# Keeping the node states of eight blocks in attention-only memory between two graph layers

## The chip, the cores and the metric

The kernel runs on one core of one Trainium2 chip. The metric is device time in microseconds (us), the median over runs of the whole program; lower is better.

The core has five engines, each with its own instruction queue. TensorE (PE, with its weight loads shown as PEld) does matrix products and transposes. VectorE (DVE) and ScalarE (ACT) do elementwise work. GpSimd (POOL) here issues the gathers and scatters, the DMAs that take row numbers from a table. SyncE (SP) issues plain DMAs. 16 DMA engines carry out what all of them issue. SBUF is the on-chip memory in 128 partitions, PSUM holds TensorE's results, HBM ("DRAM" in the code) is the memory beside the chip.

## The reference

Eight independent inputs of 2048 nodes with 128 features, all over one sparse graph (each possible edge is there with probability 1/128), pass through four layers. Layers 0 and 1 are attention over the neighbours with a feed-forward network behind it; layers 2 and 3 are graph attention with one score per edge. The text counts layers from 0, so the third and fourth layer are layers 2 and 3. Cut to what matters:

```python
# layers 0 and 1 (8 heads of 16)
Q, K, V = h @ Wq, h @ Wk, h @ Wv
attn = softmax(where(adj == 0, -inf, Q K^T / 4))
x = layer_norm(h + attn V @ Wo + bo) * g1 + b1
x = layer_norm(x + relu(x @ W1 + b1) @ W2 + b2) * g2 + b2
# layers 2 and 3
h = x @ W
e = leaky_relu(h @ a_src [i] + h @ a_dst [j], 0.2)
att = softmax(where(adj == 0, -inf, e))
y = att @ h + x                       # x, the layer's input, is added again
x = gamma * (y - mean(y)) * rsqrt(var(y) + 1e-5) + beta
```

A layer's input is thus needed twice: for its projection, and at the end of the layer, where it is added to the result. That input is what the text calls a state.

## The kernel before

**Sparse rows.** The start of the program sorts the nodes by their number of neighbours and makes a list of neighbours for each. Nodes are then worked on in 16 blocks of 128, from the most neighbours to the fewest (29 list places for block 0, 10 for block 15). Each layer has a table in HBM with one row per node, all eight inputs side by side: keys and values for layers 0 and 1 (8 KB a row), projected features and two exponentials for layers 2 and 3 (4160 bytes a row).

**Chunks.** A block's list is cut into chunks of at most 2 places (layers 0 and 1) or 4 (layers 2 and 3). For each place one gather (`gather`, L302, GpSimd) brings the rows of 128 neighbours into one of seven buffers `kv`. In layers 2 and 3 (`gat_chunk`) VectorE multiplies seven of eight inputs by the edge weights (L818), ScalarE the eighth (L823), in layer 2 VectorE also adds one pair of places (L829), and TensorE sums the places into `acc` (L316). `fetch` issues the gathers of up to five chunks ahead.

**Block ends.** After its last chunk a block has a tail (`tail`, `outputs` L703, `gat_tail`). In layer 2 it adds the state (`center` times `xT`, L852), normalizes (ACT L860, L868), transposes back, writes the new state over the old one in `xT` (L494), projects it for layer 3 (L520) and copies the result into `rows` (ACT L530), of which there is one buffer. In layer 3 it normalizes into `n`, scales and shifts it (DVE L898, L900) and writes it to the output (L902). Tails run in small steps between the chunks of the next block.

**States.** When both halves of a block are done, `state_done` stores the state to `kept[t]` in HBM (L551, SyncE), writes `rows` into the next layer's table (L507, GpSimd) and asks for the state that is needed next: block t+4 of the same layer, or of the next layer at the end (`load_state`, L298, SyncE). There are four state tiles `xT`, so a load waits until its tile's earlier block is stored and no longer read. All 16 states are stored and loaded between any two layers.

**Order.** The program's order on every engine is the order in which the Python code emits it; no scheduler moves instructions. What an engine waits for is set by semaphores derived from the tiles' use. SyncE takes its DMAs strictly in that order: one that waits holds back all behind it.

**Memory that the change touches.** The weights of layers 0 and 1 (`w_L0_...`, `w_L1_...`: `qkv`, `o`, `W1`, `w2`, together 4 KB per partition and layer), `ring` (exponentials of attention), `block_sum` (softmax sums of attention), and the pool tiles tagged `xn`, `hT` and `q`, used by attention (`q` also by layer 3's `n`, two buffers). A state takes 4 KB per partition.

Of the kernel before, what the change touches and what calls it, by code (L numbers as in the profile page):

```python
# [9 lines left out]
F32 = mybir.dt.float32  # L10
# [8 lines left out]
P = 128  # L19
B, N, D = 8, 2048, 128  # L20
# [3 lines left out]
FF = 256  # L24
# [5 lines left out]
NB = 8  # L30
# [4 lines left out]
STATES = 4  # L35
# [54 lines left out]
def sparse_path(ctx: ExitStack, tc: tile.TileContext, ins: dict, out: bass.AP, flag: bass.AP):  # L90
# [10 lines left out]
    nc = tc.nc  # L101
    const = ctx.enter_context(tc.tile_pool(name="const", bufs=1))
    work = ctx.enter_context(tc.tile_pool(name="work", bufs=2))
# [6 lines left out]
    def misc():  # L110
        return pm.tile([P, 512], F32, tag="m", name="m")
# [33 lines left out]
    bufs = [const.tile([P, CHUNK], F32, name=f"kv{i}") for i in range(KVB)]  # L145
    turn = [-1]
    ring = const.tile([P, RING, P], F32, name="ring")
# [7 lines left out]
    kept = [dram.tile([P, B * P], F32, name=f"kept{t}") for t in range(NT)]  # L155
# [19 lines left out]
    block_sum = const.tile([P, NT, NB * NH], F32, name="block_sum")  # L175
# [5 lines left out]

    waiting = []

    def load(name, shape):
        t = const.tile(shape, F32, name=f"w_{name}")
        if name == "L0_qkv":
            nc.scalar.dma_start(t, ins[name])
        else:
            waiting.append((t, ins[name]))
        return t  # L190
# [11 lines left out]
    def row(name, n):  # L202
        t = line(n)
        waiting.append((t, ins[name].rearrange("p a b -> p (a b)") if n > D else ins[name]))
        return t

    W = {}
    for l in (0, 1):
        W[l] = {
            "qkv": load(f"L{l}_qkv", [P, 384]),  # L210
            "o": load(f"L{l}_o", [P, D]),
            "1": load(f"L{l}_gnn_W1", [P, FF]),
            "2": load(f"L{l}_w2", [P, 2, D]),
            "col": load(f"L{l}_col", [P, 7]),
            "row": row(f"L{l}_row", 4 * D).rearrange("p (a b) -> p a b", b=D),
        }
# [76 lines left out]
    def state_tile():  # L293
        return work.tile([P, B, P], F32, tag="xT", name="xT", bufs=STATES)

    def load_state(t):
        xT = state_tile()
        nc.sync.dma_start(xT.rearrange("p b n -> p (b n)"), kept[t])  # L298
        return xT

# [14 lines left out]
    def turn_into(dst, src, start):  # L315
        nc.tensor.matmul(  # L316
            dst, src, ident, start=start, stop=True, is_transpose=True, skip_group_check=True
        )

    def transpose4(src):  # L320
        pt = misc()
        for j in range(4):
            nc.tensor.transpose(pt[:, j * P : (j + 1) * P], src[:, j, :], ident)  # L323
        return pt.rearrange("p (b c) -> p b c", c=P)
# [145 lines left out]
    def inverse_roots(ss):  # L470

        rs = small.tile([P, ss.shape[-1]], F32, tag="rs", name="rs", bufs=3)
        nc.scalar.activation(rs, ss, AF.Ln)
        nc.scalar.activation(rs, rs, AF.Exp, scale=-0.5)
        return rs
# [17 lines left out]
    def affine(dst, src, col):  # L493
        nc.scalar.activation(dst, src, AF.Identity, scale=col[:, 0:1], bias=col[:, 1:2])  # L494
# [11 lines left out]
    def put_rows(l, t, rows, dst=None):  # L506
        return nc.gpsimd.indirect_dma_start(  # L507
            out=tables[l][:, :] if dst is None else dst,
            out_offset=bass.IndirectOffsetOnAxis(ap=perm[:, t : t + 1], axis=0),
            in_=rows[:, : width(l)], in_offset=None,  # L510
        )
# [33 lines left out]
    def state_done(l, t, box):  # L545


        box["halves"] = box.get("halves", 0) + 1
        if box["halves"] == 2:
            if l < 3:  # L550
                nc.sync.dma_start(kept[t], box["x"].rearrange("p b n -> p (b n)"))  # L551
                dst = views[l + 1][max(0, t - (NT - LATE) + 1)]
                assert len(puts[l + 1]) == t
                puts[l + 1].append(put_rows(l + 1, t, box["rows"], dst).ins)
                put[l + 1] += 1
            box["done"] = True
            state(l, t + STATES)
# [165 lines left out]
    def rows_of(box):  # L723
        if "rows" not in box:
            box["rows"] = work.tile([P, NB * 2 * D], F32, tag="rows", name="rows", bufs=1)
        return box["rows"]

    def attention_tail(l, t, box, i):
# [54 lines left out]
        yield from project(l + 1, i, xT, rows_of(box), t)  # L783
        yield
        state_done(l, t, box)

    def gat_chunk(l, c):
# [43 lines left out]
        add_up(acc, hv, k, left, c["folded"])  # L833
        yield

    def gat_tail(l, t, box):

        wt = W[l]
        xT = box["x"]
        if l == 2:  # L840
            ns = [work.tile([P, 4, D], F32, tag="n", name="n2") for _ in range(2)]
        else:
            n = work.tile([P, NB, D], F32, tag="q", name="n")
            ns = [n[:, :4, :], n[:, 4:, :]]
        ys = [None, None]
        rs = [None, None]

        def added(h):
            ys[h] = y = misc().rearrange("p (b c) -> p b c", c=D)
            for j in range(4):  # L850
                turn_into(y[:, j, :], box["o"][:, 4 * h + j, :], j == 0)
                nc.tensor.matmul(  # L852
                    y[:, j, :], xT[:, 4 * h + j, :], center, start=False, stop=True,
                    skip_group_check=True,
                )

        def squares(h):
            ss = small.tile([P, 4], F32, tag="ss", name="ss", bufs=3)
            for j in range(4):
                nc.scalar.activation(  # L860
                    ns[h][:, j, :], ys[h][:, j, :], AF.Square, bias=eps, scale=D**-0.5,
                    accum_out=ss[:, j : j + 1],
                )
            rs[h] = inverse_roots(ss)

        def scaled(h):
            for j in range(4):
                nc.scalar.mul(ns[h][:, j, :], ys[h][:, j, :], rs[h][:, j : j + 1])  # L868

        def half_rows(h):  # L870
            scaled(h)
            yield
            pt = transpose4(ns[h])
            yield
            affine(xT[:, 4 * h : 4 * h + 4, :], pt, wt["col"][:, 0:2])
            yield
            yield from project(3, 4 * h, xT, rows_of(box), t)
            yield
            state_done(l, t, box)

        def half_done(h):
            added(h)
            yield
            squares(h)
            yield
            if l == 2:
                yield from half_rows(h)
            else:
                scaled(h)

        halves = [half_done(0), later(2, lambda: half_done(1))]
        while halves:
            advance(halves)
            yield
        if l == 3:
            for _ in range(3):
                yield
            nc.vector.tensor_mul(n, n, last_g[:, None, :].to_broadcast([P, B, D]))  # L898
            yield
            nc.vector.tensor_add(n, n, last_b[:, None, :].to_broadcast([P, B, D]))  # L900
            yield
            nc.gpsimd.indirect_dma_start(  # L902
                out=out, out_offset=bass.IndirectOffsetOnAxis(ap=perm[:, t : t + 1], axis=0),
                in_=n.rearrange("p b d -> p (b d)"), in_offset=None,
            )
            state_done(l, t, box)
            state_done(l, t, box)
# [235 lines left out]
    every = []  # L1143
    blocks = [[{} for _ in range(NT)] for _ in range(4)]
    for l in range(4):
        per = 2 if l < 2 else 4
        for t, k, ns, folded in pieces(l, per):
            c = dict(l=l, t=t, k=k, ns=ns, folded=folded, box=blocks[l][t])
# [8 lines left out]
    def advance(group):  # L1157
        for g in list(group):
            if next(g, 0) == 0:
                group.remove(g)  # L1160
# [40 lines left out]
    def later(n, make):  # L1201
        for _ in range(n):
            yield
        yield from make()

    def tail(l, t, box):
        for _ in range(4 if l < 2 else 3 if t > NT - 4 else 5):
            yield
        outputs(l, t, box)
        if l < 2:  # L1210
            tails.append(later(1, lambda: attention_tail(l, t, box, 0)))
            tails.append(later(4, lambda: attention_tail(l, t, box, 4)))
        else:
            tails.append(later(1, lambda: gat_tail(l, t, box)))
        yield

    def state(l, t):
        if t >= NT:
            l, t = l + 1, t - NT
        if 0 < l < 4:  # L1220
            blocks[l][t].update(x=load_state(t), ready=True)

    def begin(c):
        if c["l"] < 2:
# [610 lines left out]
```

## Time and profile before

| | |
|---|---|
| median of 3 runs | 2802.78 us (2800.01 to 2805.45) |
| the profiled execution | 2808.35 us, its span 2806.6 us |
| busy: PE, DVE, ACT, POOL | 84%, 90%, 49%, 63% |
| DMA | 982.02 MB, mean 350 GB/s |
| first store of a state of layer 2 | 2018.75 us |
| last load of a state of layer 3 | 2717.55 us |

The span is the time from the first to the last instruction in the profile; the execution's own time has a little around it. Times inside the profile are counted from the span's start. A row of a timeline has the start in us, the duration in us, engine, line, operation, output and input; in brackets stands the idle time of the engine before it and who ended it. A row of waits has the waiting engine and line, what it waited for, the total in us, the number of times and the longest. `issue` as a releaser means that the profile shows no wait.

In windows of the profile, layer 2's chunks run from about 1894 to 2350 us and layer 3's from about 2356 to 2766 us, with the first chunks of a layer beside the last tails of the one before.

### The profile page before, as it was taken

The numbers are of one execution on the slowest core, as the hardware profiler recorded it, in microseconds if no ns is written. First come the engines' busy times: TensorE is split into PE (matmuls) and PEld (weight loads), VectorE is DVE, ScalarE is ACT, GpSimd is POOL, SyncE is SP. The second block draws the span as 40 slices with busy tenths as digits, with TensorE's granted clock in tenths as the row PEclk, the third lists the DMA queues.
The fourth block names the chain that finished last, engine by engine and source line by source line (L and its number), as shares of the span: only waits on it lengthen the run. The fifth ranks groups of instructions, "written<-read, shape, count | busy, mean of one in ns | idle before, by whom it ended". The sixth has DMA issues, their size and how long they took to land.

```text
span 2806.6 us, 48937 instructions
## 1 busy us (share of the span) xinstructions
PE 2349.6 (84%) x17811; PEld 2130.1 (76%) x17811; DVE 2513.9 (90%) x2467; ACT 1381.9 (49%) x5032; POOL 1774.4 (63%) x1346
## 2 busy tenths in 40 slices
PE   5866898898899998798989999997767887788885
PEld 4655787787788887688878888886667786787785
DVE  9697999999999887999999999985989997799895
ACT  3611444454555665154445555565445565445554
POOL 3377788778656455546565665573776775677772
PEclk9978999999999999999999999999788888999997
DMA  9898899999989888789999999985999998999994
GB/s 368 274 370 318 358 335 331 386 334 363 382 325 365 326 329 317 304 311 367 357 386 367 354 378 363 355 324 175 382 412 385 401 409 332 349 411 413 400 413 166
DMA packets 197730, 982.02 MB, mean 350 GB/s; under 512 B 30268, under 2 KB 32060, under 8 KB 125488
## 3 DMA queue, kind: packets, MB, share of 16 engines
q0 software_dynamic: 172080, 885.06, 82.0%
q1 hardware_dynamic: 20650, 68.39, 6.3%
q10 hardware_dynamic: 4752, 25.36, 2.7%
q8 instruction: 143, 2.34, 0.3%
q14 instruction: 105, 0.86, 0.1%
HBM read 921.28 MB, written 91.55 MB: 361 GB/s over the span
## 4 chain that ended last, share of the span: by engine, by line
PE 37%; DVE 27%; DMA 15%; issue 10%; ACT 8%; POOL 2%; POOLq 0%; ACTq 0%; DVEq 0%
PE acc L316 13%; DMA kv<-table,lists 11%; DVE kv L675 9%; DVE kv L637 8%; PE pair L316 4%; PE m L773 3%; PE m L756 3%; DVE kv L818 3%; PE m L520 2%; PE m L323 2%; PE m L768 2%; PE m L573 2%; PE m L739 1%; PE m L743 1%; POOL kv L302 1%
## 5 line engine op out<-in xcount | busy, mean ns | idle before, releaser
L302 POOL DMA_INDIRECT kv<-table,lists x938 | 1305.5, 1392 | 669.3 <-PE acc L316 288.0
L316 PE MATMUL acc<-ident,kv 128*128 128x128 f32 x8048 | 1059.2, 286 | 166.5 <-DVE kv L675 90.3
L316 PEld LDWEIGHTS acc<-ident,kv 128*128 128x128 f32 x8048 | 964.3, 148 | 230.0 <-DVE kv L675 114.4
L637 DVE TENSOR_TENSOR kv<-kv,q 128x2048 f32<-128x2048 f32 (+1 forms) x280 | 617.9, 2207 | 37.2 <-DMA kv<-table,lists 26.6
L675 DVE TENSOR_TENSOR kv<-kv,weights 128x2048 f32<-128x2048 f32 (+1 forms) x282 | 625.9, 2220 | 25.1 <-ACT weights L667 24.8
L818 DVE TENSOR_TENSOR kv<-kv,pair 128x3584 f32<-128x3584 f32 (+1 forms) x150 | 530.7, 3538 | 1.0
L316 PE MATMUL pair<-ident,kv 128*128 128x128 f32 (+1 forms) x2256 | 300.2, 277 | 87.4 <-issue 75.4
L643 DVE TENSOR_TENSOR kv<-kv 128x1024 f32<-128x1024 f32 (+1 forms) x282 | 334.9, 1187 | 9.2
L316 PEld LDWEIGHTS pair<-ident,kv 128*128 128x128 f32 (+1 forms) x2256 | 255.8, 140 | 107.8 <-issue 88.3
L302 POOL DMA_INDIRECT kv<-table,sorted_lists x150 | 195.7, 1304 | 139.2 <-PE acc L316 40.8
L659 ACT ACTIVATE ring<-pair 128x128 f32<-128x128 f32 (+1 forms) x282 | 77.7, 276 | 366.5 <-PE pair L316 302.2
L823 ACT ACTIVATE kv<-kv,ws 128x128 f32<-128x128 f32 x544 | 174.7, 397 | 153.3 <-DVE ws L812 144.0
L667 ACT COPY weights<-pair 128x128 f32<-128x128 f32 (+1 forms) x282 | 73.3, 260 | 357.1 <-PE pair L663 351.4
L483 ACT ACTIVATE n<-m,eps 128x128 f32<-128x128 f32 x512 | 181.6, 371 | 135.0 <-PE m L773 130.7
L860 ACT ACTIVATE n<-m,eps 128x128 f32<-128x128 f32 x256 | 90.8, 374 | 182.2 <-PE m L852 180.0
L773 PE MATMUL m<-w_L_w,hT 128*128 128x128 f32 x1024 | 156.4, 275 | 0.0
L490 ACT ACTIVATE n<-m,rs 128x128 f32<-128x128 f32 x512 | 146.4, 376 | 0.3
L773 PEld LDWEIGHTS m<-w_L_w,hT 128*128 128x128 f32 x1024 | 135.1, 192 | 0.0
L756 PE MATMUL m<-n1T,w_L_gnn_W 128*128 128x512 f32 x256 | 132.5, 602 | 3.0 <-ACT hT L761 1.8
L703 DVE TENSOR_TENSOR o<-acc,scale 128x512 f32<-128x512 f32 x128 | 83.2, 683 | 50.5 <-ACT scale L721 27.0
L520 PE MATMUL m<-w_L_h,xT 128*128 128x130 f32 x512 | 84.8, 298 | 46.5 <-ACT xT L494 29.3
L323 PE MATMUL m<-ident,n 128*128 128x128 f32 x640 | 113.4, 290 | 11.9 <-ACT n L490 5.6
(233 smaller groups left out, 3593.2 us busy)
## 6 DMA issues: line engine op xcount, KB each, us to landing
kept<-xT SPq DMA_DIRECT2D x48, 512.0 KB, 6.7
xT<-kept SPq DMA_DIRECT2D x48, 512.0 KB, 7.0
kv<-in_adj_dram SPq DMA_DIRECT2D x16, 1024.0 KB, 15.8
table<-kv ACTq DMA_DIRECT2D x16, 1024.0 KB, 4.5
kv<-table,lists POOLq DMA_INDIRECT x938, 8.8
kv<-in_x_nodes_dram ACTq DMA_DIRECT2D x16, 512.0 KB, 11.1
kv<-table,sorted_lists POOLq DMA_INDIRECT x150, 6.7
found<-kv POOLq DMA_DIRECT2D x16, 64.0 KB, 5.6
```

The lines of the kernel that those rows point to most:

```text
L302: this = nc.gpsimd.indirect_dma_start(out=dst, out_offset=None, in_=tables[l][:, :] if need == NT else views[l][0], in_offset=bass.Indirec ...
L316: nc.tensor.matmul(dst, src, ident, start=start, stop=True, is_transpose=True, skip_group_check=True)
L323: nc.tensor.transpose(pt[:, j * P : (j + 1) * P], src[:, j, :], ident)
L483: nc.scalar.activation(dst[:, i, :], z[:, i, :], AF.Square, bias=eps, scale=D**-0.5, accum_out=ss[:, i : i + 1],)
L490: nc.scalar.mul(dst[:, i, :], z[:, i, :], rs[:, i : i + 1])
L637: nc.vector.tensor_mul(kk, kk, q[:, None].to_broadcast([P, ns, NB, D]))
L643: nc.vector.tensor_add(hk.rearrange("p j (c h) -> p c j h", h=NH), kj[:, :, :NH, :], kj[:, :, NH:, :])
L675: nc.vector.tensor_mul(vv, vv, w.rearrange("p (s b h) -> p (s b) h", b=NB, h=NH)[:, :, None, :] .to_broadcast([P, ns * NB, HD, NH]),)
L756: nc.tensor.matmul(ph, wt["1"][:, f * P : (f + 1) * P], n1T.rearrange("p b c -> p (b c)"), start=True, stop=True,)
L773: nc.tensor.matmul(y[:, j, :], hT[:, f, j, :], wt["2"][:, f, :], start=False, stop=f == 1, skip_group_check=True,)
L818: nc.vector.tensor_mul(hv[:, :, :nv, :], hv[:, :, :nv, :], wc[:, :, :nv, None].to_broadcast([P, ns, nv, D]))
L823: nc.scalar.mul(hv[:, i, b, :], hv[:, i, b, :], ws[:, i, b - nv : b - nv + 1])
```

## The change

The states of blocks 4 to 11 are loaded in layer 2 into eight places of their own, called homes: the weights of layer 0, `ring`, `block_sum`, the tiles `xn` and `hT`, both tiles `q`, and the weights of layer 1. Layer 2 updates them there, and layer 3 reads them there; their store in layer 2 and their load in layer 3 are left out (8 of each, 512 KB apiece). Blocks 0 to 3 and 12 to 15 go through `kept` as before. So that weights can hold a state, the four weight tiles of a layer become slices of one tile `every`. Layer 3's output `n`, which used the `q` tiles, goes into two halves of one tile `ends` with the tag `rows`, in turn.

```diff
+    def load(name, shape, t=None):
+        if t is None:
+            t = const.tile(shape, F32, name=f"w_{name}")
...
     for l in (0, 1):
+        every_w = const.tile([P, NB * D], F32, name=f"w_L{l}")
         W[l] = {
-            "qkv": load(f"L{l}_qkv", [P, 384]),
-            "o": load(f"L{l}_o", [P, D]),
-            "1": load(f"L{l}_gnn_W1", [P, FF]),
-            "2": load(f"L{l}_w2", [P, 2, D]),
+            "every": every_w,
+            "qkv": load(f"L{l}_qkv", None, every_w[:, :384]),
+            "o": load(f"L{l}_o", None, every_w[:, 384 : 384 + D]),
+            "1": load(f"L{l}_gnn_W1", None, every_w[:, 512 : 512 + FF]),
+            "2": load(f"L{l}_w2", None, every_w[:, 768:].rearrange("p (f d) -> p f d", d=D)),
...
+    def flat(tile):
+        return tile.rearrange("p (b n) -> p b n", n=P)
+
+    homes = [
+        lambda: flat(W[0]["every"]),
+        lambda: ring[:, :B, :],
+        lambda: flat(block_sum.rearrange("p t c -> p (t c)")),
+        lambda: work.tile([P, B, P], F32, tag="xn", name="home", bufs=1),
+        lambda: flat(work.tile([P, 2, 4, P], F32, tag="hT", name="home", bufs=1)
+                     .rearrange("p f b c -> p (f b c)")),
+        lambda: work.tile([P, B, P], F32, tag="q", name="home"),
+        lambda: work.tile([P, B, P], F32, tag="q", name="home"),
+        lambda: flat(W[1]["every"]),
+    ]
+    STAY = range(STATES, STATES + len(homes))
+
-    def load_state(t):
-        xT = state_tile()
+    def load_state(l, t):
+        xT = homes[t - STATES]() if l == 2 and t in STAY else state_tile()
         nc.sync.dma_start(xT.rearrange("p b n -> p (b n)"), kept[t])
...
             if l < 3:
-                nc.sync.dma_start(kept[t], box["x"].rearrange("p b n -> p (b n)"))
+                if l < 2 or t not in STAY:
+                    nc.sync.dma_start(kept[t], box["x"].rearrange("p b n -> p (b n)"))
...
+    ends = []
+
     def gat_tail(l, t, box):
...
-            n = work.tile([P, NB, D], F32, tag="q", name="n")
+            if not ends:
+                ends.append(work.tile([P, NB * 2 * D], F32, tag="rows", name="ends", bufs=1))
+            n = ends[0][:, t % 2 * NB * D : (t % 2 + 1) * NB * D].rearrange("p (b d) -> p b d", d=D)
...
-        if 0 < l < 4:
-            blocks[l][t].update(x=load_state(t), ready=True)
+        if l == 3 and t in STAY:
+            blocks[3][t].update(x=blocks[2][t]["x"], ready=True)
+        elif 0 < l < 4:
+            blocks[l][t].update(x=load_state(l, t), ready=True)
```

More of the change, by code (lines that the diff above doesn't have):

```diff
@@ L182, in sparse_path @@
     waiting = []
-    def load(name, shape):
-        t = const.tile(shape, F32, name=f"w_{name}")
+    def load(name, shape, t=None):
+        if t is None:
+            t = const.tile(shape, F32, name=f"w_{name}")
         if name == "L0_qkv":
```

## The prediction

> **What bounds the kernel now.** I read the page first, then windows over the two attention layers that the change touches, then what VectorE waited for in each, then GpSimd's issues.
>
> The page says that nearly everything is busy:
>
> ```profile
> span 2806.6 us, 48937 instructions
> PE 2349.6 (84%) x17811; PEld 2130.1 (76%) x17811; DVE 2513.9 (90%) x2467; ACT 1381.9 (49%) x5032; POOL 1774.4 (63%) x1346
> q0 software_dynamic: 172080, 885.06, 82.0%
> q1 hardware_dynamic: 20650, 68.39, 6.3%
> kept<-xT SPq DMA_DIRECT2D x48, 512.0 KB, 6.7
> xT<-kept SPq DMA_DIRECT2D x48, 512.0 KB, 7.0
> ```
>
> Of 96 state transfers, 16 go. Whether that is worth anything is a question to each stage, so here are the steady part of layer 2 and, in layer 3, the stretch in which the eight loads to be removed are issued (first at 2456.70, last at 2629.39):
>
> ```profile
> 2050.00:2350.00 300.00, 243.01 (x1790) 228.92 (x1789) 287.95 (x336) 175.07 (x698) 221.09 (x198) 0.88 1.00 394
> 2456.00:2650.00 194.00, 159.63 (x1340) 154.76 (x1338) 177.24 (x204) 92.84 (x360) 143.52 (x141) 0.95 1.02 410
> ```
>
> Columns: length, then PE, PEld, DVE, ACT, POOL busy, clock, DMA share, GB/s. The DMA share is full in both, so it cannot tell the two apart. What VectorE waited for does (first 2050 to 2350, then 2456 to 2650):
>
> ```profile
> DVE kv L829 <- ACT kv L823: 6.7, 8, 1.6
> DVE o L703 <- PE acc L316: 2.5, 2, 1.8
> ...
> DVE kv L806 <- DMA kv<-table,lists: 14.5, 13, 2.8
> ```
>
> Layer 2 is VectorE's: 288 of 300 us busy and not one wait for a transfer. In layer 3, without the pair addition of L829, VectorE runs ahead and waits 14.5 us for gathers. But GpSimd paces layer 3 too. Its rows there are mostly like the first and third of these:
>
> ```profile
> 2495.34 0.99 POOL L302 DMA_INDIRECT kv<-table,lists  x1 [0.30 <-issue]
> 2498.28 0.99 POOL L302 DMA_INDIRECT kv<-table,lists  x1 [1.95 <-issue]
> 2499.57 1.03 POOL L902 DMA_INDIRECT out_dram<-n,perm  x1 [0.30 <-issue]
> ```
>
> 0.99 us of work and 0.30 us between, hardly ever more: only gaps like the 1.95 us one are waiting.
>
> **The change, part by part.** Order on the engines: PE, DVE, ACT and POOL keep the same instructions in the same order; SP's queue loses 16 transfers. So nothing new is computed, and all effects come through DMA and its waits.
>
> *Eight stores of layer 2 (blocks 4 to 11) and SP's waits for them.* 8 x 0.524 MB = 4.19 MB, at 410 GB/s 10.2 us of DMA. They lie in 2134 to 2308, where VectorE waits for no transfer. Worth 0. Cover: VectorE's own 288 us; if that fell, at most 10.2 us.
>
> *Eight loads of layer 3.* The same 10.2 us of DMA, now where VectorE waits for gathers. The window was 194 us long and can shrink only to the largest of three floors. DMA: it moved 79.56 MB, less 4.19 is 75.37 MB, at 410 GB/s 183.8 us. VectorE: 194 - 14.5 = 179.5 us. GpSimd: 134 gathers and 7 output writes at 0.99 + 0.30 = 1.29 us are 181.9 us; the 3.9 us by which some issues ran beyond 0.99 (1.83 us in the longest) recur in layer 2 as well, so I leave them in: 185.8 us. GpSimd's floor is highest: at best 8.2 us come back. Three resources within 6 us of each other interfere, so I take three quarters, 6 us, with 2.5 and 10.2 as ends. What is late next is GpSimd's issue, behind it the landing. A backlog that is not there at 2650 can't push into the rest of layer 3, where four loads stay: 0.5 us.
>
> *The end of layer 2.* Store 11 (2307.55) and load 15 (2314.18) stand just before the write of rows at 2321.56, on whose landing the next copy into that one buffer (ACT L530, 2329.53) waited 2.58 us. Both leave this place; one 512 KB transfer is 1.3 us of DMA. 0.5 us, ends 0 and 1.3.
>
> *Eight loads of layer 2 change their destination, and nine change their time.* This is the part that can cost. Before, the load of block t+4 waits for block t's buffer, so SP alternates store and load, one pair every 28 us or so. After, the homes are free since layer 1 (the waits that remain are on work of layers 0 and 1), and there is no store of blocks 4 to 11 to hold SP. So as soon as the store of block 3 (2106.13) is issued, the loads of blocks 7 to 15 follow at once, blocks 12 to 15 into the tiles of blocks 0 to 3, stored by then. Nine loads, 4.72 MB, 11.5 us of DMA in one lump; nobody needs them early. Who stands beside them: gathers and row writes. Two covers:
>
> ```profile
> 2105.75 0.99 POOL L302 DMA_INDIRECT kv<-table,lists  x1 [1.41 <-PE acc L316]
> 2109.69 0.99 POOL L302 DMA_INDIRECT kv<-table,lists  x1 [0.30 <-issue]
> 2130.31 3.89 DVE L818 TENSOR_TENSOR kv<-kv,pair 128x3584 f32<-128x3584 f32 x1
> 2117.53 1.03 POOL L507 DMA_INDIRECT table<-rows,perm  x1 [0.30 <-DMA kv<-table,lists]
> 2133.24 0.38 ACT L530 COPY rows<-m 128x256 f32<-128x256 f32 x1
> 2160.58 0.39 ACT L530 COPY rows<-m 128x256 f32<-128x256 f32 x1
> ```
>
> Gathers and chunks pair off in the order of the chunk list: the four gathers that begin at 2105.75 feed the L818 at 2130.31. They were issued by 2110.7 and landed at about 2115.7, 14.6 us ahead. The tightest chunk of the next 60 us has 9.9 us. The row write of 2117.53 landed at 2124.67, 8.6 us before ACT writes that buffer again; the next (issued 2146.01, landed 2154.44) only 6.1 us before 2160.58.
>
> How far do gathers fall back? The row: one 512 KB load beside gathers takes 7.0 us, 75 GB/s. If nine went like that, they would take 63 us and leave 335 of 410 GB/s to the software queue, which asks for 347 (24.32 MB from 2100 to 2170): 0.8 MB behind, 2 us. [...] Cost: 0.5 us for what I can't see, ends 0 and 10.
>
> *Weights as slices of one tile; the output in halves of one tile.* Same transfers in the same order; the two halves serve two blocks in turn as two buffers did. 0.
>
> Sum: -6 -0.5 -0.5 +0.5 = -6.5 us. The profiled execution took 2808.35 us (span 2806.6 and 1.75 around it), 5.6 us above the median of the runs, 2802.78; a 2802 in such a profile, 2796.3 as a median.
>
> **The rivals.**
>
> *GpSimd and PE's release hold layer 3 (no change).* The gaps in GpSimd's row end with PE's accumulation, and PE waits for VectorE's products as well as VectorE for gathers. If only the long gaps near loads close, 2.5 us come back: 2800.3. For it: GpSimd is at 185.8 of 194 us. Against it: VectorE's idle time there is nearly all for gathers.
>
> *The lump (slower).* Place: layer 2, 2115 to 2190. If the backlog stays at 11.5 us over three row writes, ACT waits 11.5 less 8.6, 6.1 and 6.8 us, 13 us together. Here is what such a wait does:
>
> ```profile
> 2044.64 0.37 ACT L530 COPY rows<-m 128x256 f32<-128x256 f32 x1 [10.84 <-DMA table<-rows,perm]
> ...
> DVE kv L829 <- ACT kv L823: 7.2, 2, 6.8
> ```
>
> 10.8 us of ACT became 6.8 us of VectorE, behind which the layer's bound stands: 13 x 0.63 = 8.2 us, and 1.6 us of gathers past their 9.9. With 2.5 us gained in layer 3: 2802.8 + 9.8 - 2.5 = 2810. It decides where the backlog exceeds 6.1 us at 2155. [...]
>
> *Bytes are what counts (large gain).* 16 x 0.524 MB at 410 GB/s: 20.5 us, 2782. For it: DMA share 1.00 and 1.02. Against: no VectorE wait for DMA in layer 2 and GpSimd's pace in layer 3. Its milder form, all of 10.2 us in layer 3 plus the end of layer 2, gives 2791.
>
> *It doesn't do what it says.* A home load held up by an old reader would stall SP; every remaining wait is for work hundreds of us earlier. 1 in 100, inside the cases above.
>
> **How the numbers follow.** A measurement of this kernel can tell about 0.2%, 5.6 us, from no change. Forecast 0.53, its own range 2793 to 2800; of it 0.42 lies under 2797.2. GpSimd's pace 0.22. The lump 0.14. Bytes 0.11. So faster 0.42 + 0.11 = 0.53, same 0.11 + 0.22 = 0.33, slower 0.14. The range goes from 2787 (bytes in its milder form with some of layer 2) to 2806 (a third of the lump's price with no gain); outside are about half of bytes and most of the lump, under 0.2.
>
> **What the changed profile would show.** SP: nine loads between 2106 and about 2125, none between 2456 and about 2640. VectorE's wait for gathers in that stretch from 14.5 to 7 us or less, GpSimd nearer to 1.29 us per issue. [...] I am wrong if the stretch of layer 3 is as long as before, or if after 2115 rows of L530 or L806 show waits for DMA.

## The result, and the profile after

| | before | after |
|---|---|---|
| median of 11 runs each, side by side | 2801.15 us (2795.42 to 2805.45) | 2789.42 us (2784.41 to 2799.22) |
| ratio, 95% interval | | 0.997 [0.9959, 0.9981] |
| the profiled execution, its span | 2808.35, 2806.6 us | 2798.62, 2796.7 us |

The median is 11.7 us lower, the profiled execution 9.7 us. The ratio of 0.997 stands for 8 us, with its interval for 5 to 11. The predicted time was 2796.3 us, the range 2787 to 2806. The page of after, in the rows that were shown of before:

```profile
span 2796.7 us, 48901 instructions
PE 2345.7 (84%) x17811; PEld 2126.5 (76%) x17811; DVE 2513.7 (90%) x2467; ACT 1381.6 (49%) x5032; POOL 1755.3 (63%) x1346
q0 software_dynamic: 172080, 885.06, 82.5%
q1 hardware_dynamic: 18346, 60.00, 5.5%
kept<-xT SPq DMA_DIRECT2D x40, 512.0 KB, 6.7
xT<-kept SPq DMA_DIRECT2D x32, 512.0 KB, 8.0
home<-kept SPq DMA_DIRECT2D x4, 512.0 KB, 15.3
```

The engines' work and the gathers' queue (q0) are the same; q1 lost 8.39 MB. The shares of busy time moved by less than a point: what changed is where VectorE waited. Three windows of after: layer 2, the stretch of layer 3 in which the eight loads stood before, and the rest of layer 3 (length, then busy PE, PEld, DVE, ACT, POOL, clock, DMA share, GB/s):

```profile
2050.00:2350.00 300.00, 243.78 (x1793) 229.35 (x1791) 289.07 (x338) 176.08 (x700) 220.77 (x199) 0.88 1.00 382
2455.00:2640.00 185.00, 152.03 (x1320) 146.97 (x1317) 173.77 (x203) 91.05 (x351) 139.46 (x139) 0.98 1.02 412
2640.00:2746.00 106.00, 89.88 (x748) 88.11 (x748) 103.36 (x131) 57.92 (x233) 81.62 (x81) 0.94 1.01 398
```

VectorE's waits in layer 2 (first two rows) and in that stretch of layer 3 (last row):

```profile
DVE kv L849 <- ACT kv L843: 5.5, 8, 1.1
DVE o L723 <- PE acc L335: 2.5, 2, 1.8
...
DVE kv L826 <- DMA kv<-table,lists: 9.0, 12, 1.5
```

Layer 2 has 394 - 382 = 12 GB/s less traffic and is as long as before. In layer 3 the DMA stays full: the gathers took over what the loads left, and arrived sooner.

But the loads that are missing in layer 3 do not stand where the prediction looked for them. SyncE's loads from 2400 us on, before and after, each in one row:

```profile
2401.16 316.72 SPq L298 DMA_DIRECT2D xT<-kept  x13
2400.20 124.90 SPq L317 DMA_DIRECT2D xT<-kept  x5
```

In both, the first of the row is the load of block 3. Before, those of blocks 4 to 15 follow between 2456.7 and 2717.6. In after only blocks 12 to 15 are left to load, and nothing stands ahead of them in SyncE's queue any more. SyncE waits for the last products (L876) that read the states of blocks 0 to 3 in their tiles, and issues them at 2453.2, 2465.5, 2495.3 and 2524.8, about 200 us earlier than before. That is within 4 us of where before loads blocks 4 to 7 (2456.7, 2469.3, 2497.4, 2527.1). So up to 2530 us both kernels have the same four loads, and behind that before has eight (from 2553.9 to 2717.6) and after none. VectorE's waits for gathers in layer 3 follow this split: before up to 2532 and from there on, then after up to 2530 and from there on:

```profile
DVE kv L806 <- DMA kv<-table,lists: 4.6, 6, 1.3
DVE kv L806 <- DMA kv<-table,lists: 14.6, 11, 2.8
DVE kv L826 <- DMA kv<-table,lists: 4.7, 6, 1.3
DVE kv L826 <- DMA kv<-table,lists: 5.6, 8, 1.5
```

To see where the 9.8 us between the two traces arose, I compared the start of each chunk's large product (L818 before, L838 after), which come in the same order in both:

| chunk (layer, block, first place) | before | after | gained so far |
|---|---|---|---|
| 2, 15, 7 (end of layer 2) | 2350.7 | 2350.2 | 0.5 |
| 3, 1, 20 | 2445.0 | 2442.7 | 2.3 |
| 3, 5, 0 | 2535.0 | 2532.7 | 2.3 |
| 3, 8, 0 | 2610.0 | 2604.6 | 5.4 |
| 3, 10, 0 | 2655.4 | 2647.9 | 7.4 |
| 3, 12, 4 | 2703.6 | 2693.5 | 10.2 |
| 3, 15, 4 | 2759.3 | 2747.9 | 11.4 |
| 3, 15, 7 (last) | 2766.0 | 2756.2 | 9.8 |

From block 1 to block 5 of layer 3, with four loads in both kernels, the distance stays near 2 us. Then it grows in steps, and ahead of each of the eight larger ones (over 0.25 us) stands one of the eight loads that only before has, by 4 to 10 us in seven cases and by 25 us in the last:

| load in before at | 2553.9 | 2577.8 | 2603.5 | 2629.4 | 2654.6 | 2679.1 | 2696.5 | 2717.6 |
|---|---|---|---|---|---|---|---|---|
| step at the chunk of before at | 2560.3 | 2586.0 | 2610.0 | 2639.2 | 2662.5 | 2683.3 | 2703.6 | 2742.4 |
| gained there, us | 0.6 | 2.1 | 0.6 | 1.9 | 1.8 | 0.3 | 0.8 | 1.1 |

VectorE's waits for gathers account for nearly all of it. From the end of layer 2 to block 1 of layer 3 all its waits fell from 31.9 to 30.2 us, in the stretch where the prediction placed the eight loads its waits for gathers fell from 14.5 to 9.0 us, and after 2650 us (before) or 2642 us (after) from 4.8 to 1.0 us. The sum for the last two is 9.3 us, of which 1.5 us came back as a new wait of L723 for ScalarE. GpSimd, from the first gather of layer 3's block 2 to the last one: 317.1 us before, 309.8 after, with 10.1 and 4.6 us in which it stood idle beyond the 0.30 us between issues.

The lump of nine loads in layer 2 is there. SyncE's queue in after, with the issue of the next DMA 215 us later:

```profile
2105.46 0.32 SPq L571 DMA_DIRECT2D kept<-xT  x1
2106.07 1.98 SPq L317 DMA_DIRECT2D home<-kept  x4
2108.10 0.48 SPq L317 DMA_DIRECT2D w_L<-kept  x1
2108.68 6.33 SPq L317 DMA_DIRECT2D xT<-kept  x4
2329.77 0.32 SPq L571 DMA_DIRECT2D kept<-xT  x1
```

And it did what was feared, up to the point where it would have cost. The gathers issued at 2111.0 to 2116.6 landed at 2132.7, 16.1 us after the last issue (before: 4.9 us), 2.4 us ahead of the product that needs them (before: 13.6 us). How the two queues shared the DMA engines from 2108 to 2131 us, after (first two rows) and before (packets, MB, share of the 16 engines' time):

```profile
q0 software_dynamic: 1287, 4.76, 51.5%
q1 hardware_dynamic: 1273, 4.67, 50.7%
q0 software_dynamic: 2260, 8.36, 90.3%
q1 hardware_dynamic: 284, 1.03, 11.4%
```

The gathers' queue (q0) and the loads' queue (q1) got half each, and the gathers moved 3.6 MB less than before, which is 8.8 us at 410 GB/s. The row write beside them was late too, and ScalarE waited for it:

```profile
2116.91 1.03 POOL L526 DMA_INDIRECT table<-rows,perm  x1 [0.30 <-issue]
2135.24 0.37 ACT L549 COPY rows<-m 128x256 f32<-128x256 f32 x1 [2.46 <-DMA table<-rows,perm]
2160.00 0.38 ACT L549 COPY rows<-m 128x256 f32<-128x256 f32 x1
```

The first two rows are GpSimd's write of `rows` and the next copy into that buffer, 2.46 us late; one block later (third row) the wait is gone. VectorE lost nothing: from the chunk at 2102 us, just ahead of the lump, to the end of layer 2 the distance to before stays between 0.5 and 0.6 us. Ahead of that, where only three loads stand at other times, it had wandered between 1.6 us ahead and 2.5 us behind. A term of 2 us or less is therefore within what two single traces differ by.

### The profile page after: what moved, and what is told of

It reads as the page before. It is cut to its first block, busy times and chain, and to the rows that moved or that the text cites. A ratio compares the mean times of both kernels' runs of the same rounds, so it can differ in the third digit from the quotient of the medians.

```text
span 2796.7 us, 48901 instructions
## 1 busy us (share of the span) xinstructions
PE 2345.7 (84%) x17811; PEld 2126.5 (76%) x17811; DVE 2513.7 (90%) x2467; ACT 1381.6 (49%) x5032; POOL 1755.3 (63%) x1346
## 4 chain that ended last, share of the span: by engine, by line
PE 42%; DVE 24%; DMA 16%; issue 8%; ACT 8%; POOL 1%; ACTq 0%; POOLq 0%; DVEq 0%; SPq 0%
PE acc L335 15%; DMA kv<-table,lists 9%; DVE kv L695 8%; DVE kv L657 8%; PE pair L335 4%; PE m L793 4%; PE m L776 3%; PE m L539 3%; PE m L342 2%; DVE kv L838 2%; PE m L788 2%; PE m L593 2%; PE m L759 2%; PE m L763 2%; DMA table<-rows,perm 2%
## 5 line engine op out<-in xcount | busy, mean ns | idle before, releaser
L321 POOL DMA_INDIRECT kv<-table,lists x938 | 1282.2, 1367 | 678.0 <-PE acc L335 269.8
L838 DVE TENSOR_TENSOR kv<-kv,pair 128x3584 f32<-128x3584 f32 (+1 forms) x150 | 530.8, 3538 | 1.0
L502 ACT ACTIVATE n<-m,eps 128x128 f32<-128x128 f32 x512 | 181.5, 371 | 137.6 <-PE m L793 133.3
L843 ACT ACTIVATE kv<-kv,ws 128x128 f32<-128x128 f32 x544 | 174.5, 398 | 145.0 <-DVE ws L832 136.4
L793 PE MATMUL m<-w_L,hT 128*128 128x128 f32 x1024 | 157.3, 276 | 0.0
L793 PEld LDWEIGHTS m<-w_L,hT 128*128 128x128 f32 x1024 | 136.1, 193 | 0.0
L776 PE MATMUL m<-n1T,w_L 128*128 128x512 f32 x256 | 132.9, 604 | 3.0 <-ACT hT L781 1.8
L723 DVE TENSOR_TENSOR o<-acc,scale 128x512 f32<-128x512 f32 x128 | 83.3, 684 | 52.0 <-ACT scale L741 27.1
L526 POOL DMA_INDIRECT table<-rows,perm x57 | 82.1, 1441 | 70.1 <-ACT own L562 18.7
L342 PEld LDWEIGHTS m<-ident,n 128*128 128x128 f32 x640 | 79.6, 145 | 51.0 <-ACT n L509 23.3
## 6 DMA issues: line engine op xcount, KB each, us to landing
home<-kept SPq DMA_DIRECT2D x4, 512.0 KB, 15.3
```

The costliest lines, as they stand in the source:

```text
L321: this = nc.gpsimd.indirect_dma_start(out=dst, out_offset=None, in_=tables[l][:, :] if need == NT else views[l][0], in_offset=bass.Indirec ...
L502: nc.scalar.activation(dst[:, i, :], z[:, i, :], AF.Square, bias=eps, scale=D**-0.5, accum_out=ss[:, i : i + 1],)
L776: nc.tensor.matmul(ph, wt["1"][:, f * P : (f + 1) * P], n1T.rearrange("p b c -> p (b c)"), start=True, stop=True,)
L793: nc.tensor.matmul(y[:, j, :], hT[:, f, j, :], wt["2"][:, f, :], start=False, stop=f == 1, skip_group_check=True,)
L838: nc.vector.tensor_mul(hv[:, :, :nv, :], hv[:, :, :nv, :], wc[:, :, :nv, None].to_broadcast([P, ns, nv, D]))
L843: nc.scalar.mul(hv[:, i, b, :], hv[:, i, b, :], ws[:, i, b - nv : b - nv + 1])
```

## The experiments

The twelve runs below, of ten kernels, took place where the kernel before takes about 2910 us instead of 2801, and there the change gains nothing. The text calls this two other chips and the place of the pair the first chip; the record numbers the two, but not the first, so it can't tell a slower chip from a slower time of the same one. The first two groups ask what each part costs, and find no price for any; the last one asks what hides it there. Each group was timed beside its own runs of the kernel before.

### Undoing one part each

`a0_after` is the changed kernel. `a1_stores_back` stores blocks 4 to 11 in layer 2 as before, which also breaks up the lump; `a2_loads_back` has the eight loads of layer 3 again, into tiles that nobody reads, but not at their old times: since nobody reads the tiles, all eight follow each other between 2521 and 2559 us and those of blocks 12 to 15 between 2561 and 2610, and then none; `a3_spread` issues layer 2's loads from ScalarE's queue, where they come block by block.

```diff
# a1_stores_back
-                if l < 2 or t not in STAY:
+                if True:
                     nc.sync.dma_start(kept[t], box["x"].rearrange("p b n -> p (b n)"))
# a2_loads_back
             blocks[3][t].update(x=blocks[2][t]["x"], ready=True)
+            nc.sync.dma_start(state_tile().rearrange("p b n -> p (b n)"), kept[t])
# a3_spread
-        nc.sync.dma_start(xT.rearrange("p b n -> p (b n)"), kept[t])
+        eng = nc.scalar if l == 2 and t >= STATES else nc.sync
+        eng.dma_start(xT.rearrange("p b n -> p (b n)"), kept[t])
```

> The changed kernel again, as the yardstick for the runs beside it on this chip. Expected: 0.997 of before (2790 to 2795 us where before takes 2801), as in its first measurement.

> The changed kernel, but the states of blocks 4 to 11 are stored in layer 2 as before (nobody reads the copies). This also puts a store between any two loads on SP, so the lump of nine loads is gone. Theory (stores lie where VectorE is the bound): within 2 us of the changed kernel, about 0.997 of before. Rival (bytes count wherever they are): half of the gain is gone, 0.9985 of before. In the profile: layer 2 ends within 1 us of the changed kernel; gathers of layer 2 have 8 to 15 us between landing and use throughout.

> The changed kernel, but in layer 3 eight loads of 512 KB are issued where the loads of blocks 4 to 11 were before, into the four xT tiles, read by nobody. Theory (the loads of layer 3 are what pays): most of the gain is gone, 0.999 to 1.000 of before; what remains is 1 to 2 us from the end of layer 2. Rival (the gain comes from elsewhere, such as the end of layer 2 or the stores): 0.997 stays. In the profile: from the first gather of block 2 in layer 3 to the last gather 316 us again instead of 310.

> The changed kernel, but the twelve loads of blocks 4 to 15 in layer 2 are issued from ScalarE's queue, in its order, so they come one per block instead of nine in a lump. Theory (the lump costs nothing, since gathers land 2.4 us ahead of their use at worst): same as the changed kernel within 2 us, with a slack of 8 to 15 us restored in the profile. Rival (the lump takes a few us somewhere): 2 to 5 us less than the changed kernel, about 0.9955 of before.

Measured (the kernel before: median 2909.96 us):

| | median | ratio, 95% interval |
|---|---|---|
| a0_after | 2914.33 | 1.0020 [1.0004, 1.0037] |
| a1_stores_back | 2913.06 | 1.0013 [0.9997, 1.0028] |
| a2_loads_back | 2909.78 | 1.0006 [0.9986, 1.0026] |
| a3_spread | 2910.16 | 1.0004 [0.9986, 1.0023] |

The changed kernel itself gains nothing here, so nothing could be undone. It is even 0.2% slower than before, with an interval that leaves out 1; since the intervals of all four overlap, no part can be blamed for it. Neither the stores, nor the loads in a burst, nor the lump shows a price above 0.2%, about 6 us.

### Repeats, fewer bytes, and fewer transfers still

Two of these were repeated on the second chip. `b2_half_rows` lets layer 3's gathers bring only the second half of each row: the first half of the products is then made of old data, which changes the output and not the work. `c1_twelve` keeps twelve states on chip (blocks 0 to 7 and 12 to 15, the last four in the places that blocks 8 to 11 leave), so that only blocks 8 to 11 are stored and loaded again, and issues the loads of the homes from ScalarE's queue, which avoids the lump.

```diff
# b2_half_rows
-            out=dst, out_offset=None, in_=tables[l][:, :] if need == NT else views[l][0],
+            out=dst[:, width(3) // 2 :] if l == 3 else dst, out_offset=None, in_=tables[l][:, :] if need == NT else views[l][0],
...
-            bounds_check=N - (l < 2), oob_is_err=False,
+            element_offset=width(3) // 2 if l == 3 else 0, bounds_check=N - (l < 2), oob_is_err=False,
# c1_twelve
+    AWAY = range(2 * STATES, 3 * STATES)
...
+        if l == 2 and t >= STATES + len(homes):
+            xT = blocks[2][t - STATES]["x"]
+        elif l == 2 and t in STAY:
+            xT = homes[t - STATES]()
+        else:
+            xT = state_tile()
+        eng = nc.scalar if l == 2 and t in STAY else nc.sync
...
-                if l < 2 or t not in STAY:
+                if l < 2 or t in AWAY:
...
+        if l == 3:
+            if t not in AWAY:
+                blocks[3][t].update(x=blocks[2][t]["x"], ready=True)
+            if t in range(STATES, 2 * STATES):
+                blocks[3][t + STATES].update(x=load_state(3, t + STATES), ready=True)
```

> The changed kernel, but the states of blocks 4 to 11 are stored in layer 2 as before (nobody reads the copies), which also breaks up the lump of nine loads. On a chip where before takes about 2801 us: theory (these stores lie where VectorE is the bound) 0.997 of before, like the changed kernel; rival (bytes count everywhere) 0.9985. On a chip where before takes about 2910 us, where TensorE holds layers 2 and 3: no difference from before beyond 0.2%, by either.

> The changed kernel, but in layer 3 eight loads of 512 KB are issued where those of blocks 4 to 11 were before, into the four xT tiles, read by nobody. On a chip where before takes about 2801 us: theory (the loads of layer 3 are what pays) 0.999 to 1.000 of before, and the first to last gather of blocks 2 to 15 in layer 3 takes 316 us instead of 310; rival (the gain is from elsewhere) 0.997. On a chip of 2910 us: no difference beyond 0.2%.

> The changed kernel, but every gather of layer 3 brings the second half of each row only (2080 of 4160 bytes; what the buffer held stands in for the rest), with as many gathers. Theory (after the change GpSimd's pace of 1.29 us per issue holds layer 3, not bytes): 2 to 5 us less than the changed kernel, 0.995 to 0.9965 of before, and GpSimd's issues back to back. Rival (DMA bandwidth is still the bound): 10 to 14 us less than the changed kernel, to the floor of VectorE, 0.992 to 0.9935 of before. On a chip of 2910 us: no difference beyond 0.3%.

> A further version: twelve places on chip (the eight homes and the four xT tiles) hold the states of blocks 0 to 7 and 12 to 15 from layer 2 to layer 3; blocks 12 to 15 take the homes of blocks 8 to 11 in layer 2, whose states alone are stored and are loaded again after blocks 0 to 3 of layer 3. The loads of blocks 4 to 11 are issued from ScalarE's queue, so they come one per block. Against the changed kernel four more stores and four more loads go, all at the end of layer 2, where row writes are waited for. Theory: 2 to 4 us less than the changed kernel, 0.9955 to 0.9965 of before; if the end of layer 2 is not held by transfers, the same as the changed kernel.

Measured (the kernel before: median 2913.39 us):

| | median | ratio, 95% interval |
|---|---|---|
| a1b_stores_back | 2914.49 | 1.0000 [0.9984, 1.0016] |
| a2b_loads_back | 2916.96 | 1.0005 [0.9988, 1.0023] |
| b2_half_rows | 2910.85 | 0.9997 [0.9981, 1.0013] |
| c1_twelve | 2910.58 | 0.9988 [0.9972, 1.0004] |

`b2_half_rows` is the one that teaches: in layer 3 (2440 to 2740 us) it moved 184 GB/s where `a0_after` moved 341, with a DMA share of 0.66, and VectorE did the same 220 us of work. Half the gathers' bytes in layer 3 are worth nothing measurable on such a chip. So the removal of 4.19 MB of loads there could not be expected to gain, nor their return to cost. `c1_twelve`, the version with the least traffic, is not faster by anything measurable either.

### What holds these chips

Layers 0 and 1 take as long as on the first chip: layer 2's first product starts at 1892.2 us in `a0_after`, at 1892.6 in after. From there the distance grows, to 38 us at block 15 of layer 2, 68 us at block 3 of layer 3 and 110 us at the last chunk. Layers 2 and 3 in `a0_after`, same columns as above:

```profile
2050.00:2350.00 300.00, 227.85 (x1591) 207.58 (x1590) 262.56 (x303) 156.11 (x620) 196.81 (x182) 0.85 0.95 349
2440.00:2740.00 300.00, 230.84 (x1723) 209.53 (x1721) 219.76 (x262) 108.32 (x417) 191.83 (x190) 0.87 0.94 341
```

In the second window VectorE does 220 us of work in 300, and the DMA is no longer full. What TensorE waited for in that window says little: `issue` means that the profile shows no reason.

```profile
PEld acc L335 <- issue: 65.4, 83, 2.6
PE acc L335 <- issue: 49.7, 67, 2.4
```

Its timeline there has the longest even stretch of this kind: single matmuls 1.4 us apart with no wait on record, where the same matmuls otherwise follow each other every 0.11 us at full and every 0.21 us at half clock (the median steps in both chips' traces). The clock record has 0.54 from 2568 to 2577 us, and no matmul is missing from the trace (17811, as in before).

```profile
2571.72 0.37 PE L335 MATMUL acc<-ident,kv 128*128 128x128 f32 x1 [1.06 <-issue]
2573.13 0.37 PE L335 MATMUL acc<-ident,kv 128*128 128x128 f32 x1 [1.04 <-issue]
2574.54 0.37 PE L335 MATMUL acc<-ident,kv 128*128 128x128 f32 x1 [1.04 <-issue]
2575.94 0.58 PE L335 MATMUL acc<-ident,kv 128*128 128x128 f32 x2 [1.03 <-issue]
```

Most such steps stand alone. In layers 2 and 3 the trace of `a0_after` has 173 steps of 0.5 to 1.6 us from one matmul to the next, 159 us in all; before and after on the first chip have 44 and 47, 39 and 42 us in all. In layers 0 and 1 the three are alike (147, 153 and 140 us). The 117 to 119 us more are about the 110 us that this chip is slower by.

### Taking work off TensorE

If TensorE hides the transfers' price, a kernel that gives it less to do should bring the price out. The last four kernels leave out half of the accumulation in layers 2 and 3: of each chunk's places only the first half is added up, and the rest of the work stays. `d1_relieved` is that in the changed kernel, `d2_relieved_loads` has the loads back as well (again in a burst, the eight between 2491 and 2530 us), `d3_relieved_before` is the same edit in the kernel before, `d4_relieved_half` has the half rows.

```diff
-        add_up(acc, hv, k, left, c["folded"])
+        add_up(acc, hv, k, max(1, left // 2), c["folded"])
```

> The changed kernel, but in layers 2 and 3 TensorE adds up only half of each chunk's places (the other half is left out; gathers, VectorE's and ScalarE's work stay). This takes some 35% of TensorE's work out of these two layers, so that it can no longer hide what the transfers cost. On a chip where the kernel before takes about 2910 us: if TensorE's half clock is what the 110 us more are spent on, this comes out 60 to 110 us faster than the kernel before (2800 to 2850), and layer 3's blocks 2 to 15 take about 310 us instead of 361. If the gathers or VectorE set the pace there, it stays above 2890. On a chip where the kernel before takes about 2801 us: 2780 to 2790, since GpSimd's issues were at 95% of layer 3 there.

> As d1_relieved, with the eight loads of 512 KB back in layer 3 (into the tiles they had before the change, read by nobody). Theory: the loads cost what they keep the gathers waiting, so with TensorE out of the way this is 6 to 10 us over d1_relieved. Rival: GpSimd's own pace of issues sets layer 3 and the loads fit beside it, 0 to 2 us over d1_relieved.

> The kernel before the change with the same half of the additions left out in layers 2 and 3. Theory: d1_relieved is 6 to 10 us faster than this, and nearly all of it is the loads, so that this lies within 3 us of d2_relieved_loads. Rival (the stores of layer 2 have a price as well once TensorE is out of the way): 3 to 8 us over d2_relieved_loads. Rival (the lump of nine loads costs as soon as nothing covers it): 3 us or more under d2_relieved_loads.

> As d1_relieved, and layer 3's gathers bring only the second half of each row, which halves their bytes and leaves the number of issues. If after the change GpSimd's pace of issues (about 1.29 us from one to the next, 232 of them, 299 us) sets layer 3, this is within 3 us of d1_relieved; if bytes still set it, 10 us or more under d1_relieved.

Measured (six runs each; the kernel before: median 2916.35 us):

| | median | range | ratio, 95% interval |
|---|---|---|---|
| d1_relieved | 2874.81 | 2866.65 to 2879.89 | 0.9857 [0.9816, 0.9898] |
| d2_relieved_loads | 2873.11 | 2865.06 to 2880.66 | 0.9847 [0.9806, 0.9888] |
| d3_relieved_before | 2862.22 | 2851.89 to 2871.33 | 0.9816 [0.9774, 0.9859] |
| d4_relieved_half | 2868.09 | 2858.14 to 2873.84 | 0.9832 [0.9791, 0.9872] |

TensorE has a large part in what holds these chips: with less for it to do, all four are 42 to 54 us faster. How much the same relief gives on the first chip was not run. And my numbers failed. The relief was to give 60 to 110 us. The loads were to cost 6 to 10 us; in a burst they cost nothing (-1.7). The changed kernel was to be ahead of the one before by as much; it is 12.6 us behind. Half the bytes gave 6.7 us, with intervals that overlap.

The relief was smaller than planned, and TensorE, busy for 175 us in the window below where `a0_after` had 231, had a slower clock there; how much of the shortfall is due to that was not measured. Layer 3 in `d1_relieved` (clock in the third column from the end):

```profile
2440.00:2740.00 300.00, 175.39 (x995) 155.68 (x995) 243.61 (x287) 121.92 (x475) 202.05 (x201) 0.74 0.98 366
```

0.74 where `a0_after` had 0.87. And the lateness of TensorE remained. Here is a place in layer 2 of `d1_relieved` where its recorded work and what follows do not fit together: ScalarE waits for the products of L876, which by the record are done before 2001.5, and starts at 2014.58.

```profile
2001.03 0.39 PE L876 MATMUL m<-center,xT 128*128 128x128 f32 x2
2001.25 1.04 PE L335 MATMUL m<-ident,sums 128*128 128x128 f32 x8
2018.26 0.47 PE L335 MATMUL m<-ident,o 128*128 128x128 f32 x1 [15.97 <-ACT scale L741]
2014.58 0.37 ACT L884 ACTIVATE n<-m,eps 128x128 f32<-128x128 f32 x1 [21.61 <-remote]
2017.77 1.23 DVE L849 TENSOR_TENSOR kv<-kv 128x1024 f32<-128x1024 f32 x1 [10.07 <-ACT kv L843]
```

ScalarE waits for TensorE's semaphore alone in that instruction, and the trace has an increment of it at 2014.56. By the page a matmul's end is modelled; the increment is an event on record. So by the semaphore the products were ready 13 us after their recorded end. ScalarE's scaling L843, next in its order, came at 2016.47, and VectorE, which needed it, lost 10.07 us.

I measured this lateness at the 64 places of layers 2 and 3 where ScalarE starts the squares of half a block: how long after both the recorded end of the products and ScalarE's own instruction before it started, counted where that is over 1 us.

| trace | places over 1 us | sum |
|---|---|---|
| before, after (first chip) | 1 each of 64 | 2.0 and 3.2 us |
| a0_after, a2_loads_back, b2_half_rows | 19, 13, 22 | 91, 58, 110 us |
| the five other runs of the first two groups | 19 to 24 | 83 to 111 us |
| d3_relieved_before | 24 | 102 us (28 in layer 2, 74 in layer 3) |
| d1, d2, d4 | 31, 25, 27 | 142, 138, 141 us (57, 55, 51 in layer 2) |

The first chip has next to none of this. So on the other chips results of TensorE that come late, 58 to 142 us in all at these places, go with the time lost in layers 2 and 3. That would be why a price in transfers shows nowhere there; it is the best account of these runs, not a proof.

The 12.6 us by which the relieved kernel before is ahead stay open. Between the profiled runs of d3 and d1 the difference is 12.5 us at block 15 of layer 2 and 11.6 at the last chunk, and layer 2 has twice as much lateness in the three kernels with homes. It does not lie at the lump, which d1 issues from 2114.9: d1 is 6.4 us behind at the chunk that it starts at 2120.7, and 4.9 to 6.4 us in the 40 us after it. All three fall back by 11 to 13 us between 2004 and 2028, 90 us before the lump, and recover 2 to 5 us of it by 2047; d1 loses more between 2180 and 2260. But `d2_relieved_loads` is only 4.4 us behind at the end of layer 2 and 15.4 at the last chunk, and the four traces start layer 2 up to 7.4 us apart although the programs are equal up to there. One profile of each can't tell whether the place of the states has to do with it.

## Why the prediction was right, and where its sizes were off

The time and the direction hold, and so does the main step: in layer 3, where VectorE waits for gathers, loads that are gone let the gathers land sooner. The pair of traces on the first chip bears it out twice, since there is no gain where both kernels have the same four loads, and a step of gain after each load that only before has. It is one trace of each kernel. No run undid it: where the experiments took place the change gains nothing, and the loads came back at other times. What follows is therefore read from the two traces.

What the prediction had wrong is the order of SyncE's queue in layer 3. It let the loads of blocks 12 to 15 stay at 2654 to 2718 us ("where four loads stay") and expected no load from 2456 to about 2640. They moved up into that stretch, as the nine loads of layer 2 did, for the same reason. So the stretch lost 2.1 MB of loads instead of 4.2 (q1 moved 2.10 MB there in after, 4.19 in before), and the rest of the layer lost as much. That the term of the stretch still came out near its 6 us is in part luck, and the term behind it came out too small for this reason.

- *Eight stores of layer 2, worth 0.* Held. Layer 2 was 300 us with 288 of VectorE before and 289 after.
- *Eight loads of layer 3, 6 us (2.5 to 10.2).* In their stretch 5.1 us (2.3 to 7.4 in the table). The first three of the eight gave nothing, because blocks 12 to 14 were loaded there instead: up to 2530 us gathers landed 8.9 us after issue in both traces (medians), from there on 9.3 us in before and 7.9 in after. GpSimd's idle time came down to 4.6 us over blocks 2 to 15, so an estimate from these gaps leaves little more to gain there without fewer gathers.
- *A backlog that is not there can't push into the rest, 0.5 us.* Too small: 2.4 us between blocks 10 and 15, as VectorE's waits for gathers after the stretch fell from 4.8 to 1.0 us. No load stands there in after.
- *The end of layer 2, 0.5 us (0 to 1.3).* 1.8 us between the last chunk of layer 2 and block 1 of layer 3, above its upper end, but no more than the two traces drift apart in layer 2 ahead of the lump. It is spread over three waits of VectorE (for TensorE's sums, and for the gathers of two kinds: 0.5, 0.8 and 0.4 us). At the one buffer that I had named, the wait of 2.58 us is still 2.23 us.
- *The lump, 0.5 us (0 to 10).* It cost 0, and no run shows the 0.5 us: the distance to before stayed between 0.5 and 0.6 us from the lump to the end of layer 2. The backlog was larger than my estimate from the row, by which 75 GB/s for each load left the gathers 0.8 MB and 2 us behind. Measured were 3.6 MB: in the lump the two queues moved 4.76 and 4.67 MB in 1287 and 1273 packets, half each, so the gathers had 207 GB/s where before they had 363 (8.36 MB in those 23 us). The last of them landed 16.1 us after issue instead of 4.9, 11 us of delay at 2133. At the chunk that starts at 2162.5 it was still 3.2 us (cover 9.9 before, 6.7 after). Of the loads, the three whose landing is on record took 15.3, 21.4 and 20.9 us from issue, where a lone one took 7.0. So the cover of the chunk behind it was nearly used up: 2.4 us were left of 13.6. The lump's rival was closer than its 14 in 100 suggests: the row write's cover of 8.6 us was overrun by 2.46 us, on an engine that had the time. A wait of L530 for DMA after 2115 was one of my own signs of being wrong, and it came.
- *Weights as slices, output in halves: 0.* Nothing in the traces speaks against it.

The sum of the steps was -6.5 us, the profiled pair gives -9.8. Of the 3.3 us between them 1.9 are the term after the stretch (0.5 in the sum, 2.4 in the trace), 1.3 the layer's end (0.5 and 1.8), and 1.0 layer 2 itself, where the lump was to take 0.5 and the layer ended 0.5 earlier; the stretch came 0.9 us short. The medians differ by 11.7 us, but runs of after lie 15 us apart, so no more should be read into that.

Of the rivals, the slower lump and the full price of all bytes (2782) are out. The milder form of the latter, all of 10.2 us in layer 3 and the end of layer 2, gave 2791, which is nearer to the measured 2789.4 than my own range of 2793 to 2800. The forecast's size is thus not shown to be better than that rival's: VectorE's waits for gathers from 2530 us on fell by 9.0 us, most of the eight loads' 10.2. The wait in the stretch, which I expected at 7 us or less, was 9.0.

## What to carry to other kernels

A transfer is worth what somebody waits for it: eight loads came back as 9 us of VectorE's waits for gathers in the layer where gathers were late, while eight stores of the same size in the layer beside it were worth nothing. Transfers that were freed of their waits started earlier, so go down the whole queue and ask of each transfer that stays when it starts now: here that was nine loads in layer 2, issued within 9 us and foreseen, and four in layer 3, about 200 us earlier and not foreseen. Then look for the cover of whoever shares the DMA engines, and count it for a backlog of the whole lump. And see that the kernel before takes the same time on the chip of the experiments as in the result: where another engine sets the pace, undoing a part shows no price, and proves nothing. A transfer put back for a test needs its old waits too, or it comes at another time.

## What the runs showed of the hardware that I had not expected

- Two chips ran the same program 4% slower than the first (the kernel before 2910 and 2913 us, against 2801), all of it in layers 2 and 3, where TensorE shows 173 steps of 0.5 to 1.6 us between matmuls in `a0_after` against 44 and 47 on the first chip, among them five matmuls 1.4 us apart while the clock record says 0.54, and results that come late: up to 13 us after the recorded end in `a0_after`, up to 17 us in `d2_relieved_loads`. What TensorE is held by is not shown. The profile names it `issue`, or `remote` on the engine that waits.
- The clock record of these traces has two values, full and half, and half stood beside little work of TensorE. In before the shortest stretch of the record is 3.41 us, and the others are multiples of it within 0.1 us. The record goes to half 67 times; in nine of ten cases TensorE was busy for at most 42% of the 3.41 us ahead. It goes back 66 times, in nine of ten cases after 3.41 us with at least 90%. Where full clock went on, TensorE was busy for at least 43% of the 3.41 us ahead. In after the three shares are 43%, 88% and 44%. These are counts from two traces; what sets the clock is not shown. In layers 2 and 3 (2050 to 2350 and 2440 to 2760) half clock was granted for 117 us in before, 96 in after, 174 in `a0_after` and 325 in `d1_relieved`. From 2440 to 2740 TensorE was busy for 249 us in after, 231 in `a0_after` and 175 in `d1_relieved`, at a mean clock of 0.97, 0.87 and 0.74.
